# A four-layer network in one kernel: quantising partly on ScalarE, the residual on TensorE, banks claimed with their copies' targets, and new orders for two stages

## The chip, the cores and the metric

One core of one Trainium2 chip. The metric is the device time of one execution in microseconds (us); a kernel's time is the median over runs. Engines are named as in the profile: PE (TensorE, with PEld for its weight loads), DVE (VectorE), ACT (ScalarE), POOL (GpSimd) and SP (SyncE, which issues all the transfers here).

## The reference

Input x is (64, 128, 28, 28), float32: 64 images, 128 channels, 784 pixels. Four layers follow each other.

```
# layer 0: two 3x3 convolutions with 4-bit weights, batch norms, residual, 4-bit quantising
out = quant_act(batchnorm(conv3x3(x, quant_weight(w1))))
out = batchnorm(conv3x3(out, quant_weight(w2 * (mask2 > 0.5))))
x = quant_act(out + x)                     # round(clip(., 0, 1) * 15) / 15
# layer 1: self-attention over the 784 pixels of an image
q, k, v = Wq x + bq, Wk x + bk, Wv x + bv  # 16, 16 and 128 channels
x = gamma * (v softmax(q^T k)^T) + x
# layer 2: Mamba over the 784 pixels, 160 inner channels, 24 states
seq = layernorm(four directions of x)
delta, B, C = ...                          # from conv + silu + projections
h[t] = exp(delta[t] * A) * h[t-1] + delta[t] * u[t] * B[t];  y[t] = sum_n h[t] C[t]
x = x + scale * (fusion_w  spatial(W_out((y + D u) * silu(z))))
# layer 3: a small Mamba over 8 tokens of 16 channels at every pixel, group norm, silu, residual
x = x + silu(groupnorm(mamba(tokens of x)))
```

## The kernel before

It runs three stages one after the other.

**Convolutions** (`conv_block`, untouched): both convolutions over all images; the batch norms need all of them. Their result `c2d` lies in DRAM.

**Scan stage** (`attention_and_mamba`): layers 1 and 2 with the end of layer 0, image by image. Work of several images is in flight at once:
- `attention(b)` (tag "attend") loads c2d and x, adds them, quantises (`raw`, then `x0`, L944 to L948: Relu on ACT, then two DVE tensor_scalar, the second of which takes the rounding constant MAGIC away and divides by 15), makes `x1 = x0 + gbv` on ACT (L950), q, k and v on PE, the maximum of the scores on DVE (`mx`), the exponentials (`et`) and the weighted sum, which is added into x1; x1 is stored to `x1d`.
- `inputs(x1)` (tag "prepare") normalises and projects on PE, applies SiLU to `u` and `z` and softplus to `delta`. Each table change of ACT is bundled with its activations into one step that nothing can enter (`silus`, `together`). It stores B, C, delta and delta*u to DRAM, from where `rows_bc` and `rows_d` spread them over the partitions (`Br`, `Cr`, `dr`, `ur`), four transfers a tile.
- 30 units an image (6 groups g of 4 states, 5 quarters q of 32 channels): `inject` multiplies ur and Br on POOL into `h` (9 buffers); `decay` makes `a = exp(A * dr)` on ACT in PSUM (2 buffers of two banks each); `scan` runs the recurrence on DVE (TENSOR_TENSOR_SCAN) and multiplies the states by Cr, on POOL for 12 units (g 1, g 3, and g 5 with q 1 and q 3; `on_gpsimd`, L1233) and on DVE for 18; `sums` adds over the states on PE into `y` (one bank) and multiplies by z on DVE (`yo`).
- `after(b)` (tag "end") reloads x1 (`x1r`), projects on PE (`r`), makes `x2 = scale * (fwT r) + x1r` with one DVE scalar_tensor_tensor for each half image (L1208, L1209), stores it, and projects the inputs of the token stage (`tok`), with a SiLU bundle.
The last 3 of 8 PSUM banks (`bank`) serve all other products.

**Token stage** (`token_mamba`): layer 3. 28 groups of 1792 pixels, two halves each, four blocks a half (`block`): 8 time steps of products and sums on DVE with `h` in PSUM, factors from ACT (`a`) and POOL (`db`), sums over states on PE. It needs x2 and its projections of all images in flight.

**The order.** Both stages are recorded into a `Plan` first. `Plan.order` is a list scheduler: it prices every step (`cost`, L619), and on each engine, among the first 32 steps whose inputs are ready, takes the one of the lowest rank that can start about as soon as any. A rank is the image's (or group's) number times a constant plus a value from a table, `SCAN_PLACES` or `TOKEN_PLACES`, by the step's tag and its number in that tag (L659 to L662). What it finds is issued as a fixed order for each engine (`issue`); all recorded instructions carry the line of that call, L749. So engines run in order, and an instruction that waits holds up all behind it on its engine. A tile's buffer is taken when a step that names it starts and comes free behind its last reader; `claiming` names tiles that a step must be able to take although it does not write them (L546).

Of the kernel before, what the change touches and what calls it, by code (L numbers as in the profile page):

```python
# [16 lines left out]
F32 = mybir.dt.float32  # L17
# [3 lines left out]
ALU = mybir.AluOpType  # L21
# [206 lines left out]
class Tables:  # L228
# [20 lines left out]
    def use(self, name):  # L249
# [6 lines left out]
    None: 30.0,  # L256
    "attend": [
        131.72, 87.62, 136.36, -17.82, 42.12, -277.22, -12.91, -155.89, -116.6, -135.63, -245.25, -245.33,
        -164, -148.35, -172.02, -121.8, -166.89, -226.64, 25.69, -198.19, -16.47, -161.61, -64.43, -269.23,
        -111.62, -261.4, -375.64, -206.03, -396.49, -330.59, -141.27, -217.79, 17.12, -261.04, -89.83,  # L260
        -266.72, -199.37, -10.55, -32.32, -9.77, 59.19, -89.22, -123.68, -68.5, -197.84, -161.86, 94.13,
        -165.1, -161.14, -205.37, -435.88, -258.3, -303.79, -80.25, -260.74, -165.75, -274.89, -159.7,
        -214.68, -235.11, -191.65, -207.33, -71.38, -175, -271.34, -188.13, -85.04, -349.94, -195.93,
        -134.53, -264.18, -110.9, -23.09, -22.96, -201.74, -67.04, 22.56, -196.26, -45.59, -157.2, -160.37,
        -232.17, -144.34, -154.99, -243.45, -112.95, -95.58, -94.79, -144.21, 89.13, -321.67, -220.96,
        -267.73, -374.99, -488.01, -315.2, -792.57
    ],
    "prepare": [
        187.22, 27.22, 201.46, -7.86, -362.94, -72.62, -38.39, 5.24, -26.57, 324.79, 166.35, -68.85, 94.25,
        87.79, -241.44, -351.16, -330.42, -375.35, -424.83, -360.66, -269.71, -448.5, -243.2, -30.22,  # L270
        294.06, -23.28, -69.34, 65.01, -446.02, 4.76, -347.43, -414.88, -271.32, 20.76, 89.74, -78.29,
        99.73, 99.26, 71.66, -123.19, -289.28, -71.59, -235.96, -661.33, -557.58, -373.5, -608.33, -491.47,
        -484.59, -462.78, -44.72, -64.36, -222.82
    ],
    "inject": [
        3.23, -64.77, -109.86, -125.66, -49.06, -17.51, 66.51, 16.63, 146.97, 61.52, 128.68, 46.35, -47.99,
        -192.11, -154.41, -140.12, -57.4, -22.76, 81.73, 39.39, 33.24, -31.8, 136.82, 87.07, -56.28, -18.37,
        -132.38, -120.27, -23.1, 24.01, -180.04, -123.96, -209.72, 83.82, 201.62, 60.2, -58.81, -84.48,
        -21.01, -18.9, 52.63, -57.71, -66.48, 24.9, -58.04, -230.39, -183.2, -250.26, -219.54, -16.37,
        -104.83, -42.51, -45.17, -84.84, 16.29, 75.49, 2.4, 38.09, -17.2, 34.33, -66.02, -42.49, -91.34,  # L280
        -38.07, -0.93, -124.7, 41.07, -57.04, 42.01, 44.3, -57.4, -46.4, -25.47, -1.09, -106.49, -71.2,
        -179.91, 1.06, -46.72, 220.22, -125.02, -262.7, -267.45, -240.36, -383.84, -320.27, -642.47,
        -312.65, -573.91, -535.1, -456.52, -404.92, -695.47, -550.94, -694.4, -511.76, -585.83, -478.63,
        -496.61, -644.07, -478.01, -579.6, -362.52, -347.17, -196.73, -377.35, -542.21, -415.93, -399.76,
        -536.47, -638.39, -405.95, -618.19, -404.27, -464.98, -464.81, -412.54, -457.72, -483.5, -502.84,
        -287.59, -247.79, -565.93, -465.48, -453.06, -331.98, -171.69, -17.35, -400.94, 11.51, -130.63,
        -217.86, -287.59, -92.98, -271.6, -109.28, -164.03, -292.37
    ],
    "decay": [
        6.92, -180.19, -72.31, -116.89, -293.65, -184.54, -474.43, -94.76, -285.58, -276.45, 54.26, -142.67,  # L290
        -347.24, -277.55, -139.54, -42.67, -87.72, -225.17, -50.1, -151.15, 43.29, -49.77, 247.18, 167.66,
        197.45, 42.91, -111.63, -129.27, -296.9, -272.54, -165.49, -232.04, -246.39, -393.13, -194.4,
        -292.42, -40.37, -140.69, -270.62, -205.66, -73.54, -187.11, 269.43, 35.27, 163.98, 78.21, -77.3,
        110.88, 226.47, 68.6
    ],
    "scan": [
        25.99, 123.97, 8.95, 45.41, 392.56, -45.95, -107.69, -144.73, 94.42, 131.02, 233.89, -164.28, 28.62,
        -136.42, 15.59, 52.99, -113.39, -260.75, -10.51, 47.61, -259.44, -111.74, 42, 299.89, 342.25,
        340.75, 184.68, 1.86, 376.14, 44.49, 45.05, 68.11, 178.46, 72.96, 198.33, -26.29, 52.44, 33.91,
        190.49, 268.39, 144.22, 99.84, 437.15, 107.62, 172.73, -93.26, 69.28, -185.12, 38.43, -95.22, 89.81,  # L300
        102.2, -136.08, -141.21, 30.71, 60.85, 76.57, 125.64, 115.95, 51.17, 234.21, 91.97, -29.62, -140.52,
        50.07, 131.57, 155.86, 214.94, 228.14, 144.88, 199.13, 206.52, 149.3, 140.56, 178.57, 181.22, 87.7,
        217.11, 296.48, 89.51, 250.14, 85.71, 112.48, 238.95
    ],
    "sums": [
        7.72, -165.83, 43.41, -44.31, 93.08, 55.1, 38.25, -127.31, 84.85, 253.66, 178.81, -169.82, -92.45,
        -128.37, -598.11, -442.51, -491.37, -181.85, -650.47, -155.31, -87.72, -567.44, -89.12, -132.85,
        -272.74, -418.16, -160.73, -59.77, -374.53, -200.9, -331.61, -135.29, -160.42, -291.18, -153.54,
        -533.12, -175.82, -220.21, 245.75, 152.47
    ],  # L310
    "end": [
        -52.64, 85.96, -87.08, -316, -177.04, -176.82, 32.28, -42.34, -80.63, 169.1, 274.72, 203.22, -269.1,
        -71.14, 411.43, 373.76, 198.22, 261.22, 211.59, 385.68, -63.43, -81.97, -24.75, -70.7, -186.7,
        64.86, 95.24, 18.97, 45.75, 289.62, -183.77, 186.7, 55.05, 198, 507.42, 245.55, 242.69, 4.43,
        -30.27, 111.31, 137.74, -202.6
# [5 lines left out]
    None: 45.0,  # L321
    "xrows0": [
        -444.51, -489.62, -309.48, -154.88
    ],
    "x0": [
        -239.32, -451.51, -374.2, -311.93
    ],
    "xrows4": [
        -298.02, -196.86, -326.15, -236.59
    ],  # L330
    "x4": [
        -201.88, -245.58, -227.53, -382.46
    ],
    "xrows8": [
        -485.3, -424.67, -673.14, -212.2
    ],
    "x8": [
        -284.74, -322.99, -509.77, -239.12
    ],
    "xrows12": [  # L340
        -332.49, -226.24, -492.54, -465.04
    ],
    "x12": [
        -361.19, -229.74
    ],
    "own": [
        -293.88, -163.61, -216.79, -206.4
    ],
    "delta": [
        -417.51  # L350
    ],
    "urows0": [
        -103.39, -285.36
    ],
    "u0": [
        21.24, -143.69
    ],
    "urows4": [
        -106.33, 41.14
    ],  # L360
    "u4": [
        -220.92, -114.38
    ],
    "urows8": [
        -19.68, -61.69
    ],
    "u8": [
        -129.21, -228.88
    ],
    "urows12": [  # L370
        -152.75, -207.04
    ],
    "u12": [
        -132.69, -488.95
    ],
    "du": [
        -29.2, 10.49, -540.02
    ],
    "exps": [
        -49.7, -43.25, -27.33, -6.32, -84.59, -35.41, -17.54, -64.2, 0.67, 16.45, -2.38, -70.31, -60.96,  # L380
        -82.74, -11.59, 23.26
    ],
    "block": [
        38.81, -9.25, -55.66, 23, 22.75, 12.05, 18.5, 57.21, 20.74, 81.35, 25.45, -4.91, -29.26, -34.61,
        37.13, 20.83, 32.69, -4.71, -6.4, 50.81, -33.42, 35.11, -8.65, 18.13, -0.81, 26.26, 65.33, 63.5,
        4.11, 26.63, 20.97, 79.58, 39.84
    ],
    "rows00": [
        308, 234.51, 416.88, 292.4
    ],  # L390
    "gate00": [
        30.9, 186.35, 232.58
    ],
    "rows04": [
        220.87, 300.34, 84.88, 3.57
    ],
    "gate04": [
        272.53, 214.7, 253.18
    ],
    "rows08": [  # L400
        304.19, 278.38, 342.86, 229.71
    ],
    "gate08": [
        255.5, 303.3, 72
    ],
    "rows012": [
        295.37, 388.81, 207.89, 381.68
    ],
    "gate012": [
        162.91, 179.62, 256.82  # L410
    ],
    "rows10": [
        423.87, 416.39, 318.81, 425.99
    ],
    "gate10": [
        374.94, 338.82, 268.2, 222.48, 520.19, 492.84
    ],
    "rows14": [
        402.64, 412.85, 541.49, 426.72
    ],  # L420
    "gate14": [
        377.04, 318.84, 425.28, 470.14, 262.06, 350.98
    ],
    "rows18": [
        444.73, 450.86, 487.3, 330.79
    ],
    "gate18": [
        520.61, 282.99, 329.98, 337.01, 304.08, 515.59
    ],
    "rows112": [  # L430
        351.08, 304.57, 418.49, 483.99
    ],
    "gate112": [
        299.51, 366.13, 421.79, 335.7, 285.52, 352.41
    ],
    "norm0": [
        550.2, 484.5, 505.28, 530.77, 519.97, 421.8, 516.03, 482.12, 446.55, 356.11, 388.64, 455.42
    ],
    "norm1": [
        437.1, 435.62, 486.06, 420, 334.77, 413.26, 462.93, 288.73, 435.26, 449.72, 507.07, 441.92  # L440
    ],
    "silu": [
        652.39
    ],
    "res0": [
        524, 423.19, 488
    ],
    "res1": [
        391.36, 746.48, 789.95
    ],  # L450
    "norm2": [
        523.7, 513.47, 365.71, 341.54, 404.26, 458.53, 458.44, 408.51, 447.07, 347.67, 302.96, 274.3
    ],
    "res2": [
        640.14, 520.91, 454
    ],
}


class Recorder:  # L460


    def __init__(self, plan, engine):
        self.plan, self.engine = plan, engine
# [1350 lines left out]
```

## Time and profile before

| | us |
|---|---|
| three runs | 12047.33, 12058.29, 12060.12 (median 12058.29) |
| the profiled execution | 12061.4, of which the span of instructions is 12059.6 |
| convolutions | about 0 to 680 |
| scan stage | about 680 to 6715 |
| token stage | about 6715 to the end |
| busy in the span | PE 10261.3 (85%), DVE 10495.7 (87%), ACT 9871.0 (82%), POOL 9509.3 (79%) |
| granted TensorE clock, mean | 0.928 |

In the profile a group of instructions reads: line, engine, operation, output<-inputs by the program's names (x0, x1 and x2 all appear as x), partitions x elements, count | busy us, mean ns of one | idle us of the engine just before them and what ended it. In a list of waits: who waited <- for whom: us in total, times, the longest. Busy time of PE counts pipelined matmuls with modelled ends; a float32 matmul shows as two records.

### The profile page before, as it was taken

To read this page: it belongs to the slowest core of one execution; us is meant where nothing else is said; L and a number is where in the kernel's file an instruction comes from. 1 tells how busy PE (TensorE), PEld (TensorE's weight loads), DVE (VectorE), ACT (ScalarE), POOL (GpSimd) and SP (SyncE) were. 2 spreads that over 40 slices of the span, in tenths; PEclk is the share of its full clock that TensorE was granted. 3 is DMA by queue.
4 is the path that set the end of the run, shared out by engine and by line. 5 is a ranking of instruction groups with operands and counts; after the bars stand their busy time and mean duration, and the time that the engine had idled before them with its cause. 6 is when DMAs were issued, how large, how long until landed. Compare 5 with 4: busy or idle time off the path is not lost. (4 is left out here: it accounts for less than half of the span.)

```text
span 12059.6 us, 211949 instructions
## 1 busy us (share of the span) xinstructions
PE 10261.3 (85%) x75696; PEld 7209.1 (60%) x75696; DVE 10495.7 (87%) x10222; ACT 9871.0 (82%) x23868; POOL 9509.3 (79%) x4960
## 2 busy tenths in 40 slices
PE   9988888888888888888887688888878888888886
PEld 9744444444444444444443577777777777777776
DVE  3448998899999989888998699999999999999998
ACT  2347888888888888888886799999999999999996
POOL 0028888888888888888888688888888888888886
PEclk9989999999999999999998799999999999899998
DMA  3535555555555555555555212222122221221221
GB/s 129 197 93 158 155 155 162 164 149 157 165 157 153 163 164 149 159 163 157 153 162 149 67 50 62 60 61 63 50 66 60 60 61 53 64 63 56 61 60 52
DMA packets 758852, 1351.63 MB, mean 112 GB/s; under 512 B 212768, under 2 KB 396448, under 8 KB 757792
## 3 DMA queue, kind: packets, MB, share of 16 engines
q1 hardware_dynamic: 757792, 1338.06, 37.6%
q8 instruction: 596, 9.76, 0.3%
q14 instruction: 464, 3.80, 0.1%
HBM read 980.82 MB, written 356.65 MB: 111 GB/s over the span
## 5 line engine op out<-in xcount | busy, mean ns | idle before, releaser
L749 ACT ACTIVATE a<-delta,A 128x98 f32<-128x98 f32 x14336 | 3895.3, 368 | 43.8 <-PE y L749 38.3
L749 POOL TENSOR_TENSOR h<-ur,Br 128x784 f32<-128x784 f32 x1920 | 3543.1, 1874 | 472.2 <-PE y L749 428.8
L749 POOL TENSOR_TENSOR db<-u,BC 128x896 f32<-128x896 f32 x1568 | 3061.7, 1968 | 816.3 <-DVE h L749 802.5
L749 PE MATMUL y<-a,ident 128*128 128x112 f32 (+1 forms) x14336 | 2201.2, 318 | 639.4 <-DVE a L749 349.8
L749 PEld LDWEIGHTS y<-a,ident 128*128 128x128 f32 x14336 | 2117.5, 214 | 702.7 <-DVE a L749 367.2
L749 ACT ACTIVATE a<-dr,A 128x784 f32<-128x784 f32 x1920 | 1732.3, 915 | 528.5 <-DVE h L749 464.0
L749 DVE TENSOR_TENSOR_SCAN a<-a,h 128x784 f32<-128x784 f32 x1152 | 2050.9, 1785 | 130.1 <-ACT a L749 122.9
L749 DVE TENSOR_TENSOR_SCAN h<-a,h 128x784 f32<-128x784 f32 x768 | 1366.9, 1780 | 235.1 <-ACT a L749 226.9
L749 POOL TENSOR_TENSOR h<-h,Cr 128x784 f32<-128x784 f32 x768 | 1411.5, 1855 | 174.0 <-DVE h L749 127.9
L749 DVE TENSOR_TENSOR h<-h,a 128x896 f32<-128x896 f32 x1344 | 1476.0, 1098 | 42.0
L749 DVE TENSOR_TENSOR h<-h,db 128x896 f32<-128x896 f32 x1120 | 1230.7, 1099 | 94.3 <-DVE h L749 2.3
L749 DVE TENSOR_TENSOR h<-a,Cr 128x784 f32<-128x784 f32 x1152 | 1116.2, 971 | 137.4 <-DMA Cr<-bcd 98.6
L749 PE MATMUL y<-h,fold 128*32 128x196 f32 x15360 | 888.4, 351 | 157.5 <-POOL h L749 123.3
L749 DVE TENSOR_TENSOR a<-h,BC 128x896 f32<-128x896 f32 x896 | 976.6, 1090 | 27.4
L749 PE MATMUL y<-late,ident 128*128 128x112 f32 x7168 | 900.8, 286 | 85.4 <-DVE late L749 85.4
L749 PEld LDWEIGHTS y<-late,ident 128*128 128x128 f32 x7168 | 871.4, 202 | 104.6 <-DVE late L749 104.1
L749 PEld LDWEIGHTS y<-h,fold 128*32 128x32 f32 x15360 | 444.3, 115 | 553.3 <-POOL h L749 191.4
L749 POOL TENSOR_TENSOR xn<-s,sq 128x784 f32<-128x784 f32 x64 | 118.2, 1847 | 811.7 <-ACT sq L749 774.6
L749 PE MATMUL bank<-et,vt 112*128 112x392 f32 x1792 | 701.6, 520 | 65.0 <-ACT et L749 62.7
L749 ACT ACT_TABLE_LOAD x558 | 715.9, 1283 | 8.6
L749 PE MATMUL bank<-qt,kt 64*112 64x392 f32 x1792 | 574.9, 546 | 27.4 <-ACT et L749 20.1
L749 PE MATMUL bank<-xn,taps 128*32 128x196 f32 (+1 forms) x3072 | 527.3, 460 | 52.6 <-POOL xn L749 52.1
(207 smaller groups left out, 16999.5 us busy)
## 6 DMA issues: line engine op xcount, KB each, us to landing
Br<-bcd SPq DMA_DIRECT2D x1536, 98.0 KB, 2.7
Cr<-bcd SPq DMA_DIRECT2D x1536, 98.0 KB, 2.9
dr<-dud SPq DMA_DIRECT2D x1280, 98.0 KB, 2.4
ur<-dud SPq DMA_DIRECT2D x1280, 98.0 KB, 2.7
utd<-tok SPq DMA_DIRECT2D x128, 392.0 KB, 4.7
ztd<-tok SPq DMA_DIRECT2D x128, 392.0 KB, 3.0
rows<-utd SPq DMA_DIRECT2D x192, 256.0 KB, 2.7
xt<-in_x SPq DMA_DIRECT2D x32, 784.0 KB, 5.0
```

Source lines behind the costliest of these rows:

```text
L749: last = getattr(getattr(nc, engine), method)(*args, **kw)
```

## The change

In the scan stage:
- x0 is made by ACT: it takes MAGIC away and no longer divides by 15. x1 divides instead (scale 1/15), and the weights of q, k and v are divided by 15 once.
- x2: fwT is multiplied by `scale` once; a product of the identity with x1r goes into the same bank ahead of fwT r, and ACT copies the bank out, in place of the DVE instruction.
- `on_gpsimd`: the unit g 5, q 3 multiplies by Cr on DVE; POOL keeps 11 units.
- `claiming` is put around nine more products: each takes its bank only where the tile that the bank is copied to is free as well.
- tags: attention of images 0, 1 and all others have tables of their own ("attend0", "attend1", "attend2"), so has the preparation of image 0 ("prepare0") and the loading of its rows ("rows").

In the planner: other prices for transfers (0.46 to 0.475 us to issue, longer until landed), GpSimd, ACT with a scale per partition, tensor_scalar in SBUF and scalar_tensor_tensor. All values of SCAN_PLACES and TOKEN_PLACES are new, with 87.5 in place of 30 as the constant for each image, and 22.62 in place of 45 in the token stage (whose instructions are the same as before).

```
 SCAN_PLACES = {
-    None: 30.0,
-    "attend": [
...
+    None: 87.5,
+    "attend0": [
...
 TOKEN_PLACES = {
-    None: 45.0,
+    None: 22.62,
...
     def of(self, *chain):
 
-        self.chain = chain
+        outer, self.chain = self.chain, chain
         yield
-        self.chain = None
+        self.chain = outer
...
         if engine == "sync":
-            return 0.46, False, 2.2 + 0.018 * outs[0].partition_size() * outs[0].free_size() / 1024
+            return 0.475, False, 2.4 + 0.02 * outs[0].partition_size() * outs[0].free_size() / 1024
...
         if engine == "gpsimd":
-            return 0.12 + 0.0021 * n, True, 0.14
+            return 0.125 + 0.00215 * n, True, 0.14
...
             if hasattr(kw.get("scale"), "tensor"):
-                us += 0.09 if n > 300 else 0.135
+                us += 0.15 if n > 300 else 0.135
...
         if method == "tensor_scalar" and outs[0].space == SBUF:
-            return 0.06 + 0.00053 * n, True, 0.14
-        return 0.045 + 0.00107 * n, two, 0.14
+            return 0.06 + 0.00083 * n, True, 0.14
+        return 0.045 + 0.00107 * n + 0.06 * (method == "scalar_tensor_tensor"), two, 0.14
...
+        unmagic = wp.tile([C, 1], F32, name="unmagic")
+        nc.vector.memset(unmagic, -MAGIC)
+        of_x0 = pk[:, PK3_AT["WqT"][0] : PK3_AT["WvT"][1]]
+        nc.vector.tensor_scalar(of_x0, of_x0, 1.0 / 15.0, None, ALU.mult)
+        nc.vector.tensor_scalar(w("fwT"), w("fwT"), v("scale"), None, ALU.mult)
...
             x0 = p1.tile([C, T], F32, name="x0")
-            plan.vector.tensor_scalar(x0, raw, MAGIC, 1.0 / 15.0, ALU.subtract, ALU.mult)
+            act(x0, raw, AF.Identity, bias=unmagic)
             x1 = p2.tile([C, T], F32, name="x1")
-            act(x1, x0, AF.Identity, bias=gbv)
+            act(x1, x0, AF.Identity, bias=gbv, scale=1.0 / 15.0)
...
             sq = tmp("sq")
             for h in range(2):
                 acc = bank()[:, :HT]
-                product(acc, [(centre_w, s[:, HALF[h]])])
+                with plan.claiming(sq):
+                    product(acc, [(centre_w, s[:, HALF[h]])])
                 act(sq[:, HALF[h]], acc, AF.Square)
...
             for h in range(2):
                 acc = bank()[:, :HT]
-                product(acc, [(w("fwT"), r[:, HALF[h]])])
-                plan.vector.scalar_tensor_tensor(x2[:, HALF[h]], acc, v("scale"), x1[:, HALF[h]], ALU.mult, ALU.add)
+                with plan.claiming(x2):
+                    product(acc, [(ident, x1[:, HALF[h]]), (w("fwT"), r[:, HALF[h]])])
+                act(x2[:, HALF[h]], acc, AF.Copy)
...
         def on_gpsimd(g, q):
-            return g in (1, 3) or (g == 5 and q in (1, 3))
+            return g in (1, 3) or (g == 5 and q == 1)
 
         def attend(b):
-            x1s[b] = yield from plan.tagged("attend", b, attention(b))
+            x1s[b] = yield from plan.tagged(f"attend{min(b, 2)}", b, attention(b))
...
-        given[0] = all_of(plan.tagged("prepare", 0, inputs(x1s.pop(0))))
+        given[0] = all_of(plan.tagged("prepare0", 0, inputs(x1s.pop(0))))
```

## The prediction

> **What bounds the kernel now.** Three stages follow each other: convolutions to about 680 us, the scan stage to about 6700, the token stage to the end. I read the engines' busy time by stretches first, to see which engine is nearest to full where the work is steady.
>
> ```profile
> 2500.00:3500.00 1000.00, 889.89 (x7334) 444.37 (x7324) 904.49 (x844) 818.12 (x1214) 883.76 (x481) 0.96 0.55 158
> 3500.00:4500.00 1000.00, 890.07 (x7358) 447.02 (x7356) 905.03 (x843) 811.70 (x1211) 881.24 (x480) 0.95 0.54 158
> 4500.00:5500.00 1000.00, 892.83 (x7292) 447.87 (x7288) 898.45 (x838) 813.43 (x1208) 877.80 (x478) 0.95 0.54 157
> ```
>
> Columns after the stretch and its length: PE, PEld, DVE, ACT, POOL, the granted clock, DMA share, GB/s. No engine is full. The groups of these 3000 us hold 979 injections on POOL (h<-ur,Br) at 30 an image, so 32.63 images at a **period of 91.93 us**. Per image DVE is busy 2707.97 / 32.63 = 82.98, PE 81.91, POOL 80.99, ACT 74.87. DVE comes first, and 8.95 us of its period are idle. What ends that idle time stands in the list of waits of the same stretch:
>
> ```profile
> DVE h L749 <- ACT a L749: 113.1, 59, 3.5
> DVE h L749 <- DMA Cr<-bcd: 50.3, 42, 2.1
> DVE a L749 <- ACT a L749: 48.2, 84, 2.1
> ...
> POOL h L749 <- PE y L749: 231.4, 124, 4.3
> ```
>
> Per image: 4.94 us for decays (`a`, the exponentials of ACT), 1.54 for rows `Cr` still in transfer. POOL's largest wait is for a free `h` buffer: it runs ahead and sets nothing. The order of time shows how a decay gets late:
>
> ```profile
> 4045.13 1.28 ACT L749 ACT_TABLE_LOAD   x1
> 4046.43 1.02 ACT L749 ACTIVATE u<-u 128x980 f32<-128x980 f32 x1
> 4047.35 1.00 ACT L749 ACTIVATE z<-z 128x980 f32<-128x980 f32 x1
> 4048.37 1.28 ACT L749 ACT_TABLE_LOAD   x1
> 4049.67 0.89 ACT L749 ACTIVATE et<-bank 112x392 f32<-112x392 f32 x2
> 4050.44 1.76 ACT L749 ACTIVATE a<-dr,A 128x784 f32<-128x784 f32 x2
> ...
> 4051.46 1.79 DVE L749 TENSOR_TENSOR_SCAN h<-a,h 128x784 f32<-128x784 f32 x1 [3.13 <-ACT a L749]
> ```
>
> The SiLU bundle holds ACT for 4.5 us, two `et` copies go ahead of the next decay, and DVE, with two `a` buffers, runs dry for 3.13 us. Nothing forces the two copies (0.89 us) ahead: that is a matter of order.
>
> In the token stage (4600 us from 7100) there are 196 blocks (copies to ysb), 8 a group: 187.8 us a group. DVE is busy there 4305 us (175.7 a group), ACT 4273 (174.4). Its largest named wait, and two of its groups:
>
> ```profile
> DVE h L749 <- POOL a L749: 77.0, 32, 4.1
> ...
> L749 DVE TENSOR_TENSOR diag<-u,own 128x224 f32<-128x224 f32 x98 | 127.5, 1309 | 5.8 <-PE y L749 5.8
> L749 DVE TENSOR_TENSOR prod<-BC 128x224 f32<-128x224 f32 (+1 forms) x48 | 24.3, 535 | 1.3 <-ACT BC L749 1.3
> ```
>
> All DVE waits named there make 129 us, 5.3 a group of 24.5. A diag takes 1.309 us where prod, of the same size or twice it, takes 0.535: some 0.77 x 4 = 3.1 us a group is time inside an instruction, which hangs on what runs beside it.
>
> **The change, part by part (scan stage, per image).** Rows:
>
> ```profile
> L749 DVE TENSOR_SCALAR x<-raw 128x784 f32<-128x784 f32 x33 | 42.2, 1279 | 0.0
> L749 DVE SCALAR_TENSOR_TENSOR x<-bank,vec,x1r 128x392 f32<-128x392 f32 x66 | 40.7, 616 | 0.0
> L749 DVE TENSOR_TENSOR h<-a,Cr 128x784 f32<-128x784 f32 x588 | 570.0, 972 | 71.6 <-DMA Cr<-bcd 50.3 <-DMA dr<-dud 1.7 <-DVE h L749 1.4
> L749 ACT ACTIVATE x<-x,gbv 128x784 f32<-128x784 f32 x32 | 29.9, 936 | 0.0
> L749 PE MATMUL bank<-r,pk 128*128 128x392 f32 x132 | 70.7, 624 | 0.0
> ```
>
> 1. x0 leaves DVE (-1.279) for ACT (+0.936, the row of x1, the same shape and form). x1 keeps its cost, its scale being a constant. x0's readers on PE (27.0 us of waits for DVE x in 3000) now wait for ACT; behind a late x0 on ACT stand decays. The page Perfetto Trace Analysis of the Trainium skill (Optimizing Scalar/DVE Operations) says that DVE is the faster of the two where it has a performance mode; by it the DVE copy would cost under 0.936 and the step would give DVE at least 0.34 us less. Here the row of DVE is 1.279, so the measurement goes the other way.
> 2. The residual: two DVE instructions go (2 x 0.616 = 1.232). PE gets two more products of 128x392; r,pk has 4 matmul records an image and 70.7 / 132 = 0.536 us each, so +2.14 (1.56 by the cheapest like row, x,wz at 103.0 / 264; 2.22 by s,centre_w at 73.2 / 132). I take 2.14, the row that these products stand beside. ACT gets two copies of a bank (rd<-bank, 0.498): +0.996. The store of x2 then waits for ACT instead of DVE on SP's queue, which spends 68.5 us in 3000 on DVE x now.
> 3. One product h*Cr an image (g 5, q 3) goes from POOL (-1.855, row h<-h,Cr) to DVE (+0.972), and its decay buffer is held for that much longer.
> 4. Claims: a product takes a bank only where its copy's target is free too. No instruction changes. ACT's waits for banks (289 us in 3000, 8.9 an image) are the most this can touch, and DVE waits for a bank only 15.7 us in 3000; I cost it at nothing, both ways up to 0.5 us an image.
> 5. Scaling the weights once: two small DVE instructions, under 2 us, in front of the stage beside the load of its first image.
>
> Sums: DVE 82.98 - 1.279 - 1.232 + 0.972 = **81.44**, POOL 79.14, ACT 74.87 + 0.936 + 0.996 = **76.80**, PE **84.05**. If DVE's idle 8.95 stays, the period falls by 1.54, 64 x 1.54 = 98 us.
>
> 6. The orders. No row prices them. Bounds: DVE's waits for decays and Cr are 6.48 us an image, at best gone; at worst they grow by what ACT gains, 1.93. The planner's own prices move toward the rows: a decay 0.79 to 0.85 us (row 0.915), a transfer's landing longer, tensor_scalar 0.48 to 0.71 (rows 0.790 and 1.279), so decays and rows late by surprise should be fewer. But ACT has 1.93 us more to place. I take 2.0 of the 6.48, about the Cr rows and a tenth of the decays: 64 x 2.0 = 128 us. Token stage: at best 5.3 + 3.1 = 8.4 us a group, at worst half of the waits more (2.7). Its planner's prices hardly change, so I take 2.0: 28 x 2.0 = 56 us. Start and drain of the scan stage (680 to 840, 6600 to 6760): nothing, with 30 us either way.
>
> Sum: -98 - 128 - 56 = -282 on the profiled 12061.4: 11779. That execution is 3 us above the median of the runs, so **11776**.
>
> **Rivals.**
> A, **work only**: the order is no better, as ranks choose only among steps that are ready; the DVE work counts alone. For it: the waits follow from two `a` buffers and ACT's bundles, which stay. 12058 - 98 = 11960.
> B, **much better orders**: two thirds of both bounds: 64 x (1.54 + 4.32) = 375, 28 x 5.6 = 157: 11526. For it: the 0.89 us ahead of a decay, above. Against: ACT at 76.80 has less room.
> C, **ACT delays the decays**: its 1.93 us more all reach DVE: 81.44 + 8.95 + 1.93 = 92.32, 25 us more than now: 12083. For: the 4.94. Against: ACT idles 17 us an image now, 6.7 of them waiting for DVE to free `a` (217.5 us in 3000).
> D, **slower: TensorE sets the pace.** It is the busiest engine after the change. If its present idle time of 91.93 - 81.91 = 10.02 stays, the period is 94.07, 64 x 2.14 = 137 us longer: 12195. It decides from where PE cannot get under 7.9 us idle. For: banks and `y` come from an engine that works in order. Against: DVE waits only 52 us in 3000 for PE, and PE's own waits are for DVE, ACT and POOL. The same page (Identifying the Most-Contended Engine) holds matmul busy time for a bad measure and the weight loads' share for a good one; that is 44.6% in these rows, and by it D would not come.
>
> **How the numbers follow.** My sum 0.38 (its own range 11640 to 11900), A 0.18, B 0.17, C 0.08, D 0.19. The range 11525 to 12160 leaves out half of B and half of D. This kernel's measurement tells 0.2%, 24 us, from no change. Faster: the sum, A, B: 0.73. C lies on the border: same 0.06 with what of A and D comes near nothing, slower 0.21.
>
> **What would show it.** Period of the injections at 88.4 us (5500 to 6500 included); no x<-raw on DVE, 18 to 19 h<-a,Cr an image, POOL 79 busy; DVE's waits for Cr and decays at 4.5 an image in place of 6.5; the token group at 185.8. Wrong: PE above 95% with DVE waiting for banks or y (D), waits for ACT a above 6 us an image (C), or a token group longer than 188.

## The result, and the profile after

The changed kernel takes 11847.97 us (median of four runs, 11844.21 to 11859.45); the kernel before took 12059.21 beside it on the same chip. The ratio is **0.9825 [0.9808, 0.9842]**, 211 us less. The forecast was 11776. The profiled execution took 11844.2 us, its span 11842.3, the mean granted clock 0.938 (0.928 before).

By stages: the last scan ends at 6552.3 us (6697.7 before), so up to there 145 us are gone (forecast 98 + 128 = 226); from there to the end it is 5289.9 us (5361.9), 72 less (forecast 56). In all, 211 of the 282 us that were forecast came. First the busy time by stretches, with the columns of before (PE, PEld, DVE, ACT, POOL, granted clock, DMA share, GB/s):

```profile
2500.00:3500.00 1000.00, 902.33 (x7588) 443.23 (x7584) 925.88 (x846) 861.84 (x1284) 894.18 (x483) 0.98 0.56 162
3500.00:4500.00 1000.00, 899.37 (x7540) 439.75 (x7539) 920.14 (x840) 854.37 (x1270) 889.29 (x481) 0.98 0.56 163
4500.00:5500.00 1000.00, 899.00 (x7588) 441.75 (x7584) 927.62 (x840) 858.06 (x1276) 892.94 (x482) 0.98 0.57 163
```

The trace of after holds 1007 injections in these 3000 us, 33.57 images, so the period is 3000 / 33.57 = 89.37 us (91.93 before, 88.4 forecast). Dividing the sums of the three rows by the images gives the table.

| per image, us | before | forecast | after |
|---|---|---|---|
| DVE busy | 82.98 | 81.44 | 82.63 |
| DVE idle | 8.95 | 6.95 | 6.74 |
| ACT busy | 74.87 | 76.80 | 76.69 |
| POOL busy | 80.99 | 79.14 | 79.73 |
| PE busy | 81.91 | 84.05 | 80.45 |

DVE's idle time fell as forecast, but its busy time by 0.35 in place of 1.54. What became of the idle time stands in DVE's waits of the same stretch (who waited <- for whom: us in total, times, the longest):

```profile
DVE h L775 <- ACT a L775: 71.0, 94, 1.5
DVE a L775 <- ACT a L775: 47.9, 67, 2.5
DVE mx L775 <- PE bank L775: 47.3, 56, 1.1
DVE yo L775 <- PE bank L775: 41.7, 25, 3.8
DVE h L775 <- DMA Cr<-bcd: 0.8, 2, 0.4
```

Divided by 33.57: decays 3.54 an image (4.94), Cr 0.02 (1.54); the two waits for PE's banks are 2.65 together (`mx` and `yo`; 1.60 before). What became of the busy time stands in the groups. First two of before, then those of after:

```profile
L749 DVE SCALAR_TENSOR_TENSOR raw<-raw,s,idn 128x784 f32<-128x784 f32 x33 | 33.3, 1009 | 0.0
...
L749 DVE TENSOR_SCALAR raw<-raw 128x784 f32<-128x784 f32 x33 | 26.1, 790 | 0.0
```

```profile
L775 DVE TENSOR_TENSOR h<-a,Cr 128x784 f32<-128x784 f32 x638 | 614.8, 968 | 12.3 <-DMA Cr<-bcd 0.8 <-DVE a L775 0.2
...
L775 DVE SCALAR_TENSOR_TENSOR raw<-raw,s,idn 128x784 f32<-128x784 f32 x33 | 59.8, 1811 | 0.0
...
L775 DVE TENSOR_SCALAR raw<-raw 128x784 f32<-128x784 f32 x34 | 51.0, 1500 | 0.0
...
L775 ACT ACTIVATE x<-raw,unmagic 128x784 f32<-128x784 f32 x34 | 31.8, 934 | 13.1 <-DVE raw L775 13.1
```

No x<-raw is left on DVE, and there are 638 / 33.57 = 19.0 h<-a,Cr an image: the edit did what it says. But two instructions that it did not touch, the first DVE step of quantising (raw + idn) and the clamp (minimum and MAGIC), take 1.811 and 1.500 us where they took 1.009 and 0.790. Quantising held DVE for 1.009 + 0.790 + 1.279 = 3.08 us an image in three instructions, and now for 3.31 in two.

The added time lies inside the instructions. This table, counted from the traces, sets each of them (1500 to 6000 us) beside the POOL instruction that was running when it started:

```
                  start under a POOL instr.   end after that instr.'s end    mean us
before raw+idn     0 of 49                    -                              1.009
before clamp      49 of 49                    0.42 to 0.43                   0.790
before x0         49 of 49                    0.42 to 0.43                   1.278
after  raw+idn    50 of 50                    0.83 to 0.84                   1.81
after  clamp      50 of 50     44 of them:    0.42 to 0.43                   0.85
                                6 of them:    passed by three more (below)   6.26
```

Such an instruction ends a fixed time after a POOL instruction ends: it waits for POOL and is done 0.42 us (clamp, x0) or 0.83 (raw + idn) behind it. So of x0's row of 1.279 some 0.86 lay under POOL's instruction, and the order decides who waits. The waiting goes both ways: an injection that is issued while such a DVE instruction is at work takes 2.2 us (behind a clamp) or 2.6 (behind raw + idn) in place of 1.85.

Here is one of the 44 clamps that are done right behind the injection under way, in the timeline of POOL and then of DVE (start, us, engine, line, operation, count; a row can hold several instructions):

```profile
3424.12 1.85 POOL L775 TENSOR_TENSOR xn<-s,sq 128x784 f32<-128x784 f32 x1
3425.92 7.70 POOL L775 TENSOR_TENSOR h<-ur,Br 128x784 f32<-128x784 f32 x4
3433.55 1.87 POOL L775 TENSOR_TENSOR h<-h,Cr 128x784 f32<-128x784 f32 x1
```

```profile
3429.26 0.79 DVE L775 TENSOR_SCALAR raw<-raw 128x784 f32<-128x784 f32 x1
```

Six of the clamps waited far longer, though POOL had the same instructions before it; one of them:

```profile
3245.61 7.34 POOL L775 TENSOR_TENSOR h<-ur,Br 128x784 f32<-128x784 f32 x4
3252.92 1.83 POOL L775 TENSOR_TENSOR h<-h,Cr 128x784 f32<-128x784 f32 x1
3256.95 1.84 POOL L775 TENSOR_TENSOR h<-h,Cr 128x784 f32<-128x784 f32 x1 [2.21 <-DVE h L775]
```

```profile
3248.93 6.25 DVE L775 TENSOR_SCALAR raw<-raw 128x784 f32<-128x784 f32 x1
3255.09 1.78 DVE L775 TENSOR_TENSOR_SCAN h<-a,h 128x784 f32<-128x784 f32 x1
```

The clamp starts under the second of four injections. POOL goes on from one instruction to the next until 3254.75, and the clamp ends 0.43 us after that. POOL stopped only because its next product needs an `h` from DVE, whose scan is queued behind the clamp.

In the token stage (7100 to 11400, 4300 us) DVE's busy time fell from 4030.39 to 3988.96. Its diag and prod, first before and then after (each row mixes two shapes, 128x224 and 128x448):

```profile
L749 DVE TENSOR_TENSOR diag<-u,own 128x224 f32<-128x224 f32 x92 | 120.4, 1316 | 2.8 <-PE y L749 2.8
...
L749 DVE TENSOR_TENSOR prod<-BC 128x224 f32<-128x224 f32 (+1 forms) x46 | 23.2, 536 | 1.3 <-ACT BC L749 1.3
```

```profile
L775 DVE TENSOR_TENSOR diag<-u,own 128x448 f32<-128x448 f32 x92 | 53.6, 583 | 3.5 <-PE y L775 3.5
L775 DVE TENSOR_TENSOR prod<-BC 128x448 f32<-128x448 f32 (+1 forms) x46 | 38.4, 875 | 3.1 <-ACT BC L775 3.1
```

Of 92 diag, 52 started under a POOL instruction before and 29 after, and each takes 0.73 us less. Part of it came back in prod, which takes 0.34 more: 3 of 46 started under a POOL instruction before, and 17 after. From the first copy to ysb to the last it is 5117.7 us (5191.0 before), which is 2.6 less for each of the 28 groups.

### The profile page after: what moved, and what is told of

The parts are those of the page before. It is cut to its first block, busy times and chain, and to the rows that moved or that the text cites. A ratio compares the mean times of both kernels' runs of the same rounds, so it can differ in the third digit from the quotient of the medians.

```text
span 11842.3 us, 213623 instructions
## 1 busy us (share of the span) xinstructions
PE 10172.4 (86%) x75952; PEld 7120.7 (60%) x75952; DVE 10391.4 (88%) x10097; ACT 9983.6 (84%) x24060; POOL 9416.5 (80%) x4896
## 5 line engine op out<-in xcount | busy, mean ns | idle before, releaser
L775 POOL TENSOR_TENSOR h<-ur,Br 128x784 f32<-128x784 f32 x1920 | 3590.3, 1898 | 527.3 <-PE y L775 378.9
L775 PEld LDWEIGHTS y<-a,ident 128*128 128x128 f32 x14336 | 2157.4, 218 | 680.9 <-POOL a L775 361.4
L775 DVE TENSOR_TENSOR_SCAN a<-a,h 128x784 f32<-128x784 f32 x1216 | 2160.2, 1786 | 121.2 <-ACT a L775 106.9
L775 POOL TENSOR_TENSOR h<-h,Cr 128x784 f32<-128x784 f32 x704 | 1304.5, 1857 | 104.9 <-DVE h L775 93.7
L775 DVE TENSOR_TENSOR_SCAN h<-a,h 128x784 f32<-128x784 f32 x704 | 1252.5, 1779 | 131.1 <-ACT a L775 130.1
L775 DVE TENSOR_TENSOR h<-a,Cr 128x784 f32<-128x784 f32 x1216 | 1171.7, 968 | 24.4 <-DMA Cr<-bcd 2.1
L775 PE MATMUL y<-h,fold 128*32 128x196 f32 x15360 | 942.8, 352 | 127.4 <-DVE h L775 67.8
L775 PE MATMUL y<-late,ident 128*128 128x112 f32 x7168 | 856.2, 278 | 21.1 <-DVE late L775 21.1
L775 POOL TENSOR_TENSOR a<-a,db 128x896 f32<-128x896 f32 x224 | 469.1, 2094 | 226.7 <-issue 189.4
L775 DVE TENSOR_REDUCE mx<-bank 112x1 f32<-112x392 f32 x896 | 474.7, 555 | 111.8 <-PE bank L775 111.2
```

Of the source, the lines that this page charges most:

```text
L775: last = getattr(getattr(nc, engine), method)(*args, **kw)
```

## The experiments

Ratios are to the kernel before on the same chip; the change's own is 0.9825. Where the work of one step is exchanged, the order is made as in the changed kernel and only what the step issues is another; `issue_as` does that. So all else keeps its place on its engine. Periods and busy sums of the runs are means over 40 images from about 1700 us on; by that measure the kernel before has a period of 91.89 with DVE busy for 82.80, the change 89.56 and 82.61. Means of the clamp and of x0, and counts of images, are over 1500 to 6000 us, as in the table above. All runs but e1 and e2 contain the new order of the token stage.

### The order of the token stage, and the claims

```
 TOKEN_PLACES = {
-    None: 22.62,
+    None: 45.0,
...
+        plan.cost = plan.cost_before
```

All values of the table and the changed prices are those of before in the token stage.

> The changed kernel with the token stage in the order of before (its places and its planner's prices; the scan stage as changed). Theory: the token stage gave 72 us of the gain by its order alone (from the last scan to the end 5362 us before, 5290 after): 11848 + 72 = 11920, a group of 186.9 us, diag back at about 1.3 us on DVE. Rival: the token stage got shorter because of what precedes it (hand-over, granted clock), not by its own order: 11848 within 24, group at 184.7.

Measured: 0.9893 [0.9875, 0.9912]; the token stage is 5369.2 us long (5361.9 before, 5289.9 after), and diag is back at its old duration:

```profile
L810 DVE TENSOR_TENSOR diag<-u,own 128x224 f32<-128x224 f32 x92 | 121.7, 1330 | 2.6 <-PE y L810 2.6
```

The new token order is worth 0.9893 - 0.9825 = 0.0068, some 80 us of the 211, with the same instructions; by the two intervals it can be 50 to 110, and the trace's 5369.2 - 5289.9 gives 79. The scan stage is the change's own here, and its period is 89.35.

The claims were taken out, but for that of `tok`, without which there is no order:

```
-            with plan.claiming(nmt):
+            if True:
...
-                with plan.claiming(rq), plan.together():
+                with plan.together():
```

> The changed kernel with eight of the nine new claims taken out (that of tok stays: with these ranks no order exists without it). The planner then finds another order from the same ranks. Theory of the prediction: claims are worth nothing, within 0.5 us an image (32 us): ratio to before 0.980 to 0.985 (0.9825 as changed). Rival: the claims are what keeps banks from being held by products whose copies cannot start: ratio above 0.987, with ACT waiting longer for banks and PE for free ones.

Measured: 0.9802 [0.9786, 0.9818], period 89.84. What was expected of the planner did not happen: it found no other order. In the traces of e4 and of the change every instruction of DVE, ACT, POOL and PE and every transfer of SP stands in the same sequence. With these ranks eight of the nine claims decide nothing.

So e4 is the change measured once more, and it tells how far two measurements of one order lie apart: 0.0023 in the ratio (some 28 us). In the three traces that share the scan stage's order (the change, e1, e4) the period is 89.56, 89.35 and 89.84, and the clamp is passed by three in 6, 5 and 9 of 50 images. Differences of this size between the runs below show nothing.

### The moves in the old order

```
+            plan.issue_as(("scalar", "activation", (x0, raw, AF.Identity), dict(bias=unmagic)))
...
+                plan.issue_as(
+                    ("tensor", "matmul", (acc,), dict(lhsT=ident, rhs=x1[:, HALF[h]], start=True, stop=False)),
+                    ("tensor", "matmul", (acc,), dict(lhsT=w("fwT"), rhs=r[:, HALF[h]], start=False, stop=True)),
+                )
...
+                plan.issue_as(("scalar", "activation", (x2[:, HALF[h]], acc, AF.Copy), dict()))
```

The order is that of the kernel before, and the unit g 5, q 3 stays on POOL.

> The kernel before with its own planned orders, in which x0 is issued on ACT and the residual by PE and an ACT copy (two of the three moves; claims, tags and orders as before). Theory of the prediction: DVE loses 1.279 + 1.232 = 2.51 us an image and its waits stay: 64 x 2.51 = 161 us less, ratio to before 0.987. Rival: an order planned for other durations can't use it, ACT's 1.93 us more delay decays and PE's 2.14 delay the banks: ratio 0.998 to 1.006. So far two kernels in which work moved without a new plan (min on POOL, old work in the new order) came out slower, which speaks for the rival.

Measured: 1.0016 [1.0007, 1.0025]. The row of its windows for the steady stretch:

```profile
2500.00:5500.00 3000.00, 2687.52 (x22056) 1343.04 (x22054) 2634.82 (x2412) 2485.26 (x3718) 2637.32 (x1434) 0.97 0.54 157
```

DVE's busy time is 2634.82 us (2707.96 before), 80.79 an image and so 2.0 less. The period is 92.10: all of it became idle time. Its waits:

```profile
DVE h L753 <- ACT a L753: 108.9, 45, 3.5
DVE yo L753 <- PE y L753: 68.3, 67, 2.4
DVE h L753 <- DMA Cr<-bcd: 60.4, 44, 2.9
DVE a L753 <- ACT a L753: 52.3, 96, 2.1
DVE mx L753 <- PE bank L753: 38.0, 65, 0.9
```

Waits for PE (`yo` and `mx`) are 106.3 us in 3000, twice the 52.1 of before, and Cr gives 60.4 (50.3). The waits for decays are 161.2, as before (161.3). So the rival's number came, and of its two reasons the one on PE's banks is seen, while ACT's added work delayed no decays. In this order, which was made for the old work, work taken from the busiest engine gave no time.

### The old work in the new orders

```
+            plan.issue_as(("vector", "tensor_scalar", (x0, raw, MAGIC, 1.0, ALU.subtract, ALU.mult), dict()))
...
+                plan.issue_as(("vector", "scalar_tensor_tensor", (x2[:, HALF[h]], acc, v("scale"), x1[:, HALF[h]], ALU.mult, ALU.add), dict()))
...
+            if (g, q) == (5, 3):
+                plan.issue_as(("gpsimd", "tensor_tensor", (h, h, Cr, ALU.mult), dict()))
```

> The changed kernel's planned order with the old work in it: x0 on DVE, the residual by DVE's scalar_tensor_tensor with one product on PE, unit g 5 q 3 multiplied on POOL. Rival, the prediction's price: the moves take 1.54 us an image off DVE, so 98 us come back: 11946. Theory, port: the 1.279 us of x0 in the profile of before were 0.42 us of work and the rest a wait for POOL, which in the changed kernel is paid by raw instead; the moves are worth the 0.35 us an image by which DVE's busy time fell, up to 0.7: 11870 to 11893. If the moves had cost time, it is below 11848.

Measured: 0.9982 [0.9969, 0.9994], period 92.64, neither of the expected numbers. The clamp takes 5.23 us in the mean, since in 32 of 48 images POOL passes it three times more; DVE's busy time is 87.11. The scan stage is longer than before's (its last scan ends at 6731.8 us, against 6697.7); the ratio is under 1 only by the token stage, 5288.4 us here. So the orders could not be priced alone. Two runs part the three moves. In the first only x0 is back on DVE (the first line of the diff):

> The changed kernel in its own orders, x0 alone issued on DVE again. Theory, POOL's train: x0 or the tensor_scalar on raw starts under an instruction of POOL and is passed over by those that follow back to back, 5 us an image and more as in the two kernels with the old work; the period goes to 92 or beyond, ratio to before 0.995 or more. Rival, the prediction's price: x0 is 1.279 us of DVE work an image, 82 us, ratio 0.989.

Measured: 0.9845 [0.9828, 0.9861], period 89.57. The clamp takes 1.47 us, DVE is busy 83.02, and x0 takes 0.768 (min/median/max ns in the instruction view of tile `raw`):

```profile
L779 DVE TENSOR_SCALAR x<-raw x34: 534/797/832, 2533.7 to 5491.7; 128x784 f32<-128x784 f32 x34
```

In 44 of 50 images it starts under a POOL instruction and takes 0.80; in the other six it waits for nobody and takes 0.534. Both expectations fall: in this order x0's move is worth nothing that can be told from the change. In the second x0 stays on ACT, and the residual and the unit are as before (the other lines of the diff):

> The changed kernel in its own orders with two of the three moves undone: the residual on DVE again (one product less on PE) and unit g 5 q 3 on POOL; x0 stays on ACT. Theory: these moves are worth nothing by themselves, the order brought the gain: ratio to before within 0.980 to 0.986. Rival: POOL's 1.86 us and DVE's 1.23 us an image were needed: 0.988 or more.

Measured: 0.9961 [0.9948, 0.9974], period 92.33. The theory's 0.980 to 0.986 falls. The rival's number, 0.988 or more, came, but not by the prices that it names. The same view shows why:

```profile
L779 DVE TENSOR_SCALAR raw<-raw x32: 3355/7034/7631, 2572.0 to 5436.2; 128x784 f32<-128x784 f32 x32
```

The clamp is now passed by three in 47 of 49 images and DVE is busy for 88.20 us. That is 5.6 more than in the change, and the clamp alone takes 5.5 more. What POOL runs behind the clamp is the same as in the change (two more injections and a product without a gap); why it is passed here in nearly every image and there in 6 of 50, the traces do not show.

### The clamp on other engines

The change's DVE is the busiest, so if its sum sets the pace, the clamp should pay on POOL:

```
+            plan.issue_as(("gpsimd", "tensor_scalar", (raw, raw, 15.0, MAGIC, ALU.min, ALU.add), dict()))
```

> The changed kernel's order, but the clamp and rounding of raw (tensor_scalar min, add) is issued on POOL in place of DVE. Theory, port and DVE sets the pace: DVE loses 1.50 us an image (0.42 of work, the rest waiting), 64 x 1.5 = 96 us: 11752, while raw + idn on DVE keeps its 1.8 us. Rival: DVE's busy time isn't what sets the period after the change (PE, or ACT's decays): 11848 within 24, with DVE's idle time longer by 1.5 us. Second rival: POOL's own instruction is long (over 3 us) and the scan is late: above 11870.

Measured: 0.9925 [0.9910, 0.9940], slower than the change; period 91.56 with DVE busy at only 81.28. The second rival's time came, with POOL's instruction just under its 3 us, over three times the 0.85 that most clamps take on DVE:

```profile
L779 POOL TENSOR_SCALAR raw<-raw x33: 2826/2827/2828, 2563.2 to 5493.8; 128x784 f32<-128x784 f32 x33
```

DVE's waits for decays rise to 224.9 + 52.5 = 277 us in 3000 (119 in the change). With raw + idn taken away as well, as a scaling on ACT and a sum on POOL,

```
+            plan.issue_as(("scalar", "activation", (raw, raw, AF.Identity), dict(scale=s2)), ("gpsimd", "tensor_tensor", (raw, raw, idn, ALU.add), dict()))
```

> As e8, and raw * s2 + idn also leaves DVE: ACT multiplies by s2, POOL adds idn. Theory, port and DVE sets the pace: DVE loses 1.50 + 1.81 = 3.31 us an image, at most 212 us: 11636; less where ACT (0.94 more) delays decays: I expect 11690. Rival: POOL, with some 1.85 + 1.85 us more an image, then sets the pace (79.8 + 3.7 = 83.5 of 89.5 us): 11850 or more.

it comes to 0.9968 [0.9959, 0.9978], period 92.48, DVE 79.49, POOL 83.36. In these two runs DVE has less to do and the kernel is slower: DVE's sum is not the pace. POOL's sum rises in both, though it fills only 90% of the period. That lateness on one engine of a fixed order reaches the others would explain it; which step is late was not traced.

### Without the clamp

What does the clamp cost in all? It is left out of the change's order:

```
-        nc.vector.memset(unmagic, -MAGIC)
+        nc.vector.memset(unmagic, 0.0)
...
+            plan.issue_as()
```

> The changed kernel's order with DVE's tensor_scalar on raw (clamp and rounding) left out, so x0 isn't quantised; nothing takes its place. Theory: DVE's busy time and its waits inside instructions set the period: 1.5 us an image less, 64 x 1.5 = 98 us, ratio to before 0.974. Rival: the period is held by how the engines' fixed orders interlock, not by DVE's sum: 0.980 to 0.983, DVE idle 1.5 us an image more.

Measured: 0.9793 [0.9778, 0.9807], period 89.02, DVE busy 81.19. Of 1.50 us of DVE's work only 89.56 - 89.02 = 0.54 of period comes back, and DVE idles 0.88 us more: nearer to the rival than to the theory. And left out of the old work in the new orders (x0 there is a tensor_scalar that subtracts 0):

> The kernel with the old work in the new orders (x0 and residual on DVE, one more unit on POOL), again with the tensor_scalar on raw left out. There this instruction took 5.29 us an image, as POOL's back-to-back instructions passed it three times over. Theory: that wait is what made the old work 189 us slower in the new orders; without it the difference to the kernel without clamp but with the new work is the moves' own price, 0.7 to 1.5 us an image: ratio 0.004 to 0.008 above that kernel's. Rival: the old work itself costs that much there: the difference stays near 0.0157.

Measured: 1.0111 [1.0096, 1.0126], period 95.58, slower by 0.032 than e10 where much less was expected. The wait moved to the next instruction of the same form: x<-raw takes 6.90 us in the median. So leaving the clamp out did not price the orders either.

### The clamp off the shared port

If the clamp waits for something that it shares with POOL, another shape of the same work might not. x0 was tried first: on DVE, with `raw` in 7 rows of 112 that have a gap between them, read in two dimensions and written to a contiguous tile:

```
+            raw = p2.tile([C, 7, 113], F32, name="raw", tag="raw", bufs=1)[:, :, :112]
...
+            plan.issue_as(("vector", "tensor_scalar", (rows7(x0), raw, MAGIC, 1.0, ALU.subtract, ALU.mult), dict()))
```

> As the kernel with x0 alone on DVE, but raw lies in 7 rows of 112 with a gap behind each and x0 in one piece, so that x0's instruction runs over unlike patterns and should read and write through DVE's own port alone. Theory, POOL's train: x0 then takes 0.9 to 1.0 us flat (like h<-a,Cr, 0.968 for as many elements), it waits for no POOL instruction, and the ratio comes back to 0.982 to 0.987. Rival: the long instruction isn't a wait for a port shared with POOL: x0 stays as long as without the gaps, ratio 0.995 or more.

Measured: 0.9875 [0.9860, 0.9890]. x0 takes the same time whatever POOL does:

```profile
L779 DVE TENSOR_SCALAR x<-raw x33: 935/944/945, 2543.1 to 5431.2; 128x784 f32<-128x784 f32 x33
```

But it took 0.768 in its plain form, so for x0 the shape costs more than it saves. The clamp is a control here: it reads and writes the rows with gaps, alike on both sides, and it still waits for POOL. It is passed by three in 10 of 50 images and takes 1.96 us in the mean (1.47 in e5), which is part of the slower time. So the gaps alone do not take the wait away; unlike sides do. Then the clamp itself:

```
-            raw = tmp("raw")
+            raw_ = p2.tile([C, 7 * 113], F32, name="raw", tag="raw", bufs=1)
+            raw, apart = raw_[:, :T], raw_.rearrange("p (a b) -> p a b", b=113)[:, :, :112]
...
-            plan.vector.tensor_scalar(raw, raw, 15.0, MAGIC, ALU.min, ALU.add)
+            plan.vector.tensor_scalar(apart[:, ::-1, ::-1], rows7(raw)[:, ::-1, ::-1], 15.0, MAGIC, ALU.min, ALU.add)
...
-            act(x0, raw, AF.Identity, bias=unmagic)
+            act(rows7(x0), apart, AF.Identity, bias=unmagic)
```

> The changed kernel with the tensor_scalar on raw (clamp and rounding) writing into 7 rows of 112 with gaps (backwards, in place), so that it should use DVE's own port alone. Theory: 0.9 to 1.0 us flat in place of 0.8 to 6.3 (mean 1.5); at most what leaving it out gave (0.5 us an image): ratio 0.978 to 0.982. Rival: the pattern isn't single-port, or the backward form is slower: 0.9825 or more.

Measured: **0.9799 [0.9784, 0.9813]**, 11800.83 us, period 88.99. Tile `raw` in its instruction view, and below it the same instruction of the change:

```profile
L775 DVE TENSOR_SCALAR raw<-raw x34: 957/958/960, 2512.2 to 5450.9; 128x784 f32<-128x784 f32 x34
```

```profile
L775 DVE TENSOR_SCALAR raw<-raw x34: 779/830/6281, 2541.9 to 5490.6; 128x784 f32<-128x784 f32 x34
```

With the same work at the same place in the same order, the reshaped clamp takes 958 ns every time and waits for no POOL instruction, though it starts under one in all 51 images (1500 to 6000 us). This run beats the kernel before clearly. That it beats the change is not shown: the change's order, measured again as e4, gave 0.9802. The only sign of a lead is that the period of 88.99 lies 0.36 below the lowest of the three traces with the change's own scan stage (89.35).

So the wait belongs to the form of the instruction, not to its place, its data or POOL's load. That it is a wait for a port is what the Trainium skill gives as a rule (SBUF — State Buffer, SBUF: two separate sides): DVE in a two-port mode, or with two SBUF inputs, and GpSimd lock one pair of ports for a whole instruction, and the other engine "fully blocks". The traces agree with the lock (the ends 0.42 and 0.83 us behind POOL's) and go beyond it: in 6 of 50 images of the change the waiting DVE instruction is passed by three further POOL instructions. The Trainium skill also has the condition that the reshaped clamp does not meet (VectorE: DVE Perf Modes, Mode 2×_2P: the outermost dimension of both sides even, or odd and equal; here one side has 7 rows and the other runs through); the 0.958 without a wait agrees with it.

## Why the prediction was right, and where it was not

**The time.** 11848 lies near the sum's 11776 and inside its own range, 11640 to 11900. Of its terms, DVE's work was to give 98 us and gave 64 x 0.35 = 22; the scan stage's idle time was to give 128 and gave 64 x 2.21 = 141; the token stage was to give 56 and gave 72. (The first two make 163, and the last scan ends only 145 earlier: the other 18 are lost outside the 3000 us from which the two are worked out.) So the terms for the two orders came in size, and the term of DVE's work did not. The orders' terms had no row behind them, and that they came so near is in part luck, as 6 shows.

**1 to 3, DVE's work, -1.54 us an image, -98 us: the step that failed.** The durations were read as work. x0's 1.279 held some 0.75 of waiting for POOL (the shortest in e5 is 0.534), and with x0 gone the raw instructions wait instead: +0.80 and +0.71. Busy time fell by 0.35. The second half of the step, that the period falls with DVE's sum, was wrong as well in the old order: there the two moves took 2.0 us from DVE and the ratio was 1.0016. What step 1 made of the page Perfetto Trace Analysis of the Trainium skill (Optimizing Scalar/DVE Operations) turns around too: by its rule the DVE copy costs less than ACT's 0.936. The row of before (1.279) spoke against that, but beside other POOL instructions the same copy took 0.768.

**The sums of the other engines.** ACT came as worked out (76.80, measured 76.69) and POOL nearly so (79.14, 79.73; an injection takes 1.901 us, 1.875 before, which is 0.8 an image, as injections now wait for raw + idn). PE went the other way: 80.45 against 84.05. The two new products do cost 64.2 / 136 x 4 = 1.89 us an image (2.14 taken, group bank<-x1r,ident), but the rest of PE's work took 3.3 us less, beside a granted clock of 0.98 in place of 0.95 to 0.96.

**4 and 5, the claims and the weights, nothing.** Right for eight claims: without them the order is the same (e4). Whether they helped in finding the ranks, no run shows. The weights were not tried alone; the first scan starts at 827 us, at 824 before.

**6, the orders.** Scan stage: 2.0 us of DVE's idle time were taken, 2.21 came. The Cr waits went almost entirely, as thought. Decays gave 1.40, where a tenth of them, 0.5, was taken, and the waits for PE's banks, which were taken at nothing, took 1.05 back; that the two nearly cancel is luck. Whether the orders give this by themselves is **open**: with the old work they meet the passed clamp (e3, e12) or its successor (e11), and neither an order searched for the old work in this planner nor the old work with the reshaped clamp of e16 in the new orders was tried. What the runs do show is that in the scan stage neither half paid alone as it was tried: the moves in the old order gave 1.0016, the new orders on the old work ended the stage later than before (6731.8 us), and both together ended it 145 us earlier. Token stage: 56 taken, 72 in the trace and about 80 by e1. Most is not waiting, which even grew (POOL a from 68.7 to 95.6 us in that stretch), but diag's time beside POOL, the 3.1 us a group that the prediction named as the most there was to gain of that kind: 4 x (1.316 - 0.583) = 2.9 came, of which 2 x 0.34 = 0.7 went back to prod, for which the prediction had no term. Another 8 x 0.157 = 1.3 came from h<-a,db (1.240 us, 1.397 before), of which 44 of 186 start under a POOL instruction, in place of 82 of 184.

**The rivals.** A (11960, work only) falls: the work alone brought nothing (e2) and the idle time did move. B (11526) asked for twice the idle time. C (ACT delays the decays) falls in the change, with waits for decays at 3.54, under the 6 that would have shown it, and in e2, where they stayed as they were. D (TensorE sets the pace) did not come: PE is at 90%, not over 95, though the waits for its banks did grow to 2.65 us an image. The prediction's 0.2% for what can be told from no change is as much as two measurements of one order differ by (e4).

**In which images POOL passes the clamp** is **open**. POOL having work without a gap is not enough: in all 50 images of the change the next injection follows without one, and 44 clamps are done at the end of the injection under way. Nor does the place decide: those 44 start in the median 1.48 us into the injection, and the six that are passed 1.44 to 1.49. In e12 they start earlier, 0.06 to 0.77 us into it, and 47 of 49 are passed; whether that is the cause was not tried.

## What to carry to other kernels

Before a duration is counted as work, set each such instruction beside what the other engine was running: a fixed distance from the other engine's end means that part of it is waiting, and moving the instruction away can hand the wait to the next one of its kind, as here. In this kernel, issued in a fixed order, work that was moved brought nothing in the order made for the old work; price the two together, not as a sum. Where an instruction is held up by back-to-back work of another engine, try another shape for it: here it took 0.958 us every time, in place of 0.78 to 6.28 with a mean of 1.50. What that is worth in time is not shown. And measure one order twice before reading small differences between orders: here two measurements differ by 0.0023.

## What the runs showed of the hardware that was not expected

- A DVE tensor_scalar that waits for POOL is not always served at the end of the POOL instruction under way. In 44 of 50 images of the change it was, and POOL's next injection then took 2.2 us in place of 1.85. In 6 it was passed by three more and took 6.26 us (7.03 in the median of e12, where 47 of 49 were passed), until POOL itself waited for DVE, with a gap of 2.2 us.
- The same tensor_scalar of 128x784 f32 takes 2.83 us on POOL (e8), where a tensor_tensor of that size takes 1.83 to 1.9.
- The granted TensorE clock in the scan stage rose from 0.95 to 0.96 before to 0.98 after, while PE's busy share rose only from 89 to 90%.
